# A four-layer network on one core: layer 0's scan taken two pixel tiles at a time, with its small work spread over other engines

## The chip, the cores and the metric

The kernel runs on one core of a Trainium2 chip. Five engines work side by side, each through its own queue in order: TensorE (PE; its weight loads are listed as PEld), VectorE (DVE), ScalarE (ACT), GpSimd (POOL) and SyncE (SP, which here only starts DMA transfers). The metric is the device time of the whole program in microseconds (us), as the median of several runs.

## The reference

One image x of 1024 channels by 64 x 64 pixels goes through four layers, each added to its input. Layer 0 is the one that changes:

```python
def layernorm2d(x):                       # over the 64 x 64 pixels of a channel
    return (x - mean) / sqrt(var + 1e-5) * w + b
x_norm = layernorm2d(group_norm(x))       # groups of 32 channels
dt     = softplus(einsum('bsdc,c->bsd', x_norm, dt_w) + dt_b)     # per channel s, image row d
log_a  = dt * -exp(log_A)
M      = exp(cumsum(log_a)[t] - cumsum(log_a)[j])  for j <= t, else 0
x      = x + einsum('btjr,bjrc->btrc', M, x_norm)
```

The sum over j with M is a recurrence along the channels: for each pixel, state[t] = exp(log_a[t]) * state[t-1] + x_norm[t]. Layer 1 is a group norm and a 1024 x 1024 product over the channels. Layer 2 has products, a scan whose order comes from sorting scores of the pixel positions, and gather and scatter by that order. Layer 3 is another 1024 x 1024 product.

## The kernel before

The products of layers 1 to 3 take nearly all the time, on TensorE. Layer 0 comes first and is all vector work. It is cut into 8 units, u = 0 to 7: unit u holds 256 channels (chunk c = u // 2, two tiles of 128 channels, k = 0 and 1) and half the image rows (h = u % 2), 2048 pixels. An even unit lies in a tile `low`, an odd one in `image`, which stays in SBUF for layer 1. A unit is worked in 4 pieces (g), a piece being 4 tiles of 128 pixels, so there are 32 pieces, i = 4u + g. A piece goes through these steps:

- unit_stats (L550): bn_stats on VectorE, 512 pixels each, 16 to a unit. norm_chunk (L558) makes a chunk's scale and bias: a chain VectorE, TensorE (L202), VectorE, TensorE (L211), VectorE, ScalarE (L172, L173), VectorE.
- normalize (L568): ScalarE writes xn, 1024 pixels at a time (L575).
- turn_in (L581): TensorE transposes eight 128 x 128 blocks into PSUM, so that pixels lie on partitions and channels along the row (L590). Four copies with weight and bias bring them to the piece's XT (10 buffers), on ScalarE (L598) or, for tiles named in `share`, on VectorE (L596).
- row_dt (L600): four matmuls sum a row's pixels with dt_w, into PD of the unit (L606). Each f32 matmul shows as two instructions.
- decay (L608), once per unit. Step 0: four ScalarE operations for the two parts of softplus (L615 to L618). Step 1: VectorE adds the parts (L621). Step 2: ScalarE makes a = exp(-exp(log_A) * dt) in PSUM (L624).
- scan (L626): four tensor_tensor_scan on VectorE, one for each pixel tile, over 256 channels (L632). From unit 2 on they start from `carry`, the last state of unit u - 2. hand_on (L635) copies the new last states to carry: VectorE for units 0 and 1, GpSimd after that (L638).
- turn_back (L641): TensorE transposes into two PSUM banks `pb` (L646). add_up (L649): VectorE adds each bank to the image in place and gives its sum for layer 1's norm (L656).
- squares (L659): ScalarE sums the squares for layer 1's variance, 1024 pixels at a time (L671), 512 in the last unit.

The order on VectorE, ScalarE, GpSimd, TensorE and SP is the program's own here (L513). The loop over the pieces (L722) is software-pipelined: in turn i it issues normalize(i+9), scan(i), hand_on(i), add_up(i-1), turn_in(i+7), row_dt(i+6), turn_back(i), then statistics of later units, a step of a norm chain, squares of the unit before, and a step of `sums`. The sums are GpSimd's: sums and differences of weight blocks for later layers (sum_weights, L440). They have a period of four pieces: at g = 0 four loads on GpSimd's queue (L448), at g = 2 four operations (L454 to L457), at g = 3 four stores (L460). The loads must wait for the stores before them.

Units come in by SP: cst and par (constants) first, then units 0 to 5 and 7; unit 6 at piece 8, when its buffer is free. The buffer is that of unit 0, whose result keep(0) writes out at piece 4. A table `spec`, which only layer 2 reads, is filled on GpSimd and stored by SP (L240) at the start. make_scores (L251) computes the positions' scores in small VectorE operations, in between the first norm chain and before it; sort_work (L328) sorts them during layer 1.

After the last piece, L770 to L775 make mean1 and var1, and pointwise (L952) the norm chain `gnl`. Then ScalarE writes normalized tiles (b, t; L948) for layer 1's matmuls (L844); VectorE makes differences of them (L802) and takes the products out of PSUM (L963, L967). Layer 1 has 56 products of eight matmuls, and the loop at L993 counts them as i. SP loads their weights (L827) into five buffers. In layer 1 only VectorE, TensorE, GpSimd and ScalarE keep the program's order; the scheduler places SP's transfers.

## Time and profile before

| | us |
|---|---|
| median of 3 runs (lowest, highest) | 2684.88 (2682.02, 2690.34) |
| the profiled execution | 2685.99 |
| its span in the trace | 2684.1 |
| first xn (L575) starts | 28.23 |
| first scans of pieces 0, 2, 4, 8, 12, 16, 20, 24, 28 start | 53.98, 69.31, 82.67, 102.65, 128.41, 149.56, 167.73, 185.42, 201.13 |
| last scan ends, layer 1's first matmul starts | 215.1, 225.07 |

Engine shares over the span: PE 96%, DVE 68%, ACT 40%, POOL 45%. In the profile's lines a group is: line, engine, operation, out<-in with shapes, count, busy us and mean ns of one, then idle time just before and who ended it. A timeline line gives start and duration in us, engine, line, operation, operands, count, and in brackets the wait before it with its releaser. Instructions of one engine overlap a little at their ends, so I take prices from the distance of starts. A stretch line gives its bounds, its length, each engine's busy us (and instructions), the granted TensorE clock, the DMA share and GB/s.

### The profile page before, as it was taken

The numbers are of one execution on the slowest core, as the hardware profiler recorded it, in microseconds if no ns is written. First come the engines' busy times: TensorE is split into PE (matmuls) and PEld (weight loads), VectorE is DVE, ScalarE is ACT, GpSimd is POOL, SyncE is SP. The second block draws the span as 40 slices with busy tenths as digits, with TensorE's granted clock in tenths as the row PEclk, the third lists the DMA queues.
The fourth block names the chain that finished last, engine by engine and source line by source line (L and its number), as shares of the span: only waits on it lengthen the run. The fifth ranks groups of instructions, "written<-read, shape, count | busy, mean of one in ns | idle before, by whom it ended". The sixth has DMA issues, their size and how long they took to land.

```text
span 2684.1 us, 30608 instructions
## 1 busy us (share of the span) xinstructions
PE 2564.7 (96%) x9520; PEld 1712.4 (64%) x9520; DVE 1833.2 (68%) x3870; ACT 1079.5 (40%) x1835; POOL 1215.3 (45%) x1100
## 2 busy tenths in 40 slices
PE   4788999999999999999999999999999999899998
PEld 3674444444555555444454448888888888788887
DVE  7996866655555564367787775677585775877877
ACT  3783110103556564466767663332233223312120
POOL 4154123242132243146474635566575565554544
PEclk9897999999999999999999999999999999999999
DMA  7245467547565577487667946889899798888896
GB/s 291 99 169 204 138 239 251 174 150 241 142 175 142 139 194 179 123 267 238 206 208 237 311 152 199 235 254 293 227 304 259 245 309 220 270 293 297 301 315 213
DMA packets 422741, 597.22 MB, mean 223 GB/s; under 512 B 141972, under 2 KB 210707, under 8 KB 419508
## 3 DMA queue, kind: packets, MB, share of 16 engines
q1 hardware_dynamic: 298020, 367.89, 43.4%
q10 hardware_dynamic: 91456, 136.33, 14.5%
q0 software_dynamic: 33104, 91.04, 13.3%
q8 instruction: 77, 1.26, 0.2%
q14 instruction: 84, 0.69, 0.1%
HBM read 435.10 MB, written 160.05 MB: 222 GB/s over the span
## 4 chain that ended last, share of the span: by engine, by line
PE 80%; DVE 10%; ACT 6%; DMA 2%; issue 1%; POOL 0%; DVEq 0%; ACTq 0%; SPq 0%; POOLq 0%
PE mm L844 36%; PE q_P5P L1728 5%; PE q_P6P L1728 5%; PE q_P7P L1728 5%; PE q_P3P L1728 5%; PE q_P4P L1728 5%; PE q_P2P L1728 5%; PE q_P1P L1728 5%; PE py L1375 2%; PE l2pt L1090 2%; DVE xt L632 1%; DVE cvp L1071 1%; DVE stats L554 1%; ACT b L948 1%; ACT xt L598 1%
## 5 line engine op out<-in xcount | busy, mean ns | idle before, releaser
L844 PE MATMUL mm<-t,w 128*128 128x512 f32 x1536 | 683.9, 596 | 0.0
L844 PE MATMUL mm<-b,w 128*128 128x512 f32 x1152 | 514.4, 598 | 4.0 <-ACT b L948 2.9
L844 PEld LDWEIGHTS mm<-t,w 128*128 128x128 f32 x1536 | 286.9, 191 | 323.1 <-issue 316.3
L844 PEld LDWEIGHTS mm<-b,w 128*128 128x128 f32 x1152 | 216.0, 191 | 252.3 <-issue 241.3
L1384 POOL DMA_INDIRECT y_rows<-g,dst x74 | 73.3, 990 | 184.3 <-ACT g L1380 171.7
L1071 DVE SCALAR_TENSOR_TENSOR cvp<-xs,par,cvp 128x512 f32<-128x512 f32 x128 | 95.3, 753 | 76.8 <-ACT cvp L1068 74.5
L1697 ACT COPY qQ<-q_P5P 128x512 f32<-128x512 f32 x48 | 28.1, 585 | 295.1 <-PE q_P5P L1728 288.8
L468 POOL TENSOR_TENSOR s<-s 128x256 f32<-128x256 f32 (+3 forms) x120 | 129.9, 1088 | 7.5
L1378 ACT COPY g<-py 8x512 f32<-8x512 f32 x146 | 83.8, 574 | 107.5 <-PE py L1375 101.7
L1122 DVE TENSOR_TENSOR xs<-mm,xs 128x512 f32<-128x512 f32 x64 | 41.8, 684 | 116.1 <-PE mm L844 116.1
L1098 POOL TENSOR_TENSOR acc<-l2xt,acc 128x136 f32<-128x136 f32 x56 | 27.8, 497 | 192.4 <-ACT l2xt L1092 191.4
L963 DVE SCALAR_TENSOR_TENSOR image<-mm,par,image 128x512 f32<-128x512 f32 x64 | 47.1, 746 | 96.4 <-PE mm L844 96.4
L1090 PEld LDWEIGHTS l2pt<-both,cv 128*128 128x128 f32 x512 | 76.3, 190 | 36.2 <-issue 22.5
L802 POOL TENSOR_TENSOR t<-t,b 128x512 f32<-128x512 f32 x40 | 55.7, 1419 | 91.8 <-DVE t L802 91.7
L1496 ACT ACTIVATE qb<-x_x_b,gn_bias,gn_r_r 128x512 f32<-128x512 f32 x64 | 48.8, 807 | 113.2 <-DVE qQ L1658 37.3
L948 ACT ACTIVATE b<-image,gnl_bias,gnl_r_r 128x512 f32<-128x512 f32 x48 | 37.2, 808 | 141.6 <-PE mm L844 113.3
L1728 PE MATMUL q_P1P<-t_b,wq_P1P 128*128 128x256 f32 x384 | 92.3, 385 | 1.5 <-POOL t_b L1492 1.5
L1728 PE MATMUL q_P4P<-t_t,wq_P4P 128*128 128x256 f32 x384 | 90.9, 380 | 1.4 <-DVE qV L1705 1.4
L1728 PE MATMUL q_P6P<-t_t,wq_P6P 128*128 128x256 f32 x384 | 90.8, 379 | 0.2 <-DMA wq_P6P<-s_d 0.2
L1728 PE MATMUL q_P5P<-t_t,wq_P5P 128*128 128x256 f32 x384 | 90.8, 379 | 0.0
L1728 PE MATMUL q_P7P<-t_t,wq_P7P 128*128 128x256 f32 x384 | 90.7, 379 | 0.0
L1728 PE MATMUL q_P2P<-t_b,wq_P2P 128*128 128x256 f32 x384 | 90.7, 379 | 0.0
(418 smaller groups left out, 5906.7 us busy)
## 6 DMA issues: line engine op xcount, KB each, us to landing
w<-s_d SPq DMA_DIRECT2D x96, 512.0 KB
w<-in_w_dram SPq DMA_DIRECT2D x72, 512.0 KB
x_x_b<-x_d ACTq DMA_DIRECT2D x28, 1024.0 KB
image<-x_d SPq DMA_DIRECT2D x12, 2048.0 KB
wq_P6P<-s_d SPq DMA_DIRECT2D x84, 256.0 KB
wq_P7P<-s_d SPq DMA_DIRECT2D x84, 256.0 KB
wq_P5P<-s_d SPq DMA_DIRECT2D x84, 256.0 KB
wq_P3P<-s_d SPq DMA_DIRECT2D x84, 256.0 KB
```

The costliest lines, as they stand in the source:

```text
L468: eng.tensor_tensor(out, a, b, ALU.subtract)
L802: eng.tensor_tensor(B[name][k], B[one][k], B[two][k], ALU.subtract)
L844: nc.tensor.matmul(to[o], w[:, k, o * P : (o + 1) * P], B[name][k], start=(fresh and k == 0), stop=(k == KH - 1), skip_group_check=True)
L948: nc.scalar.activation(t, X[nb][:, ct, :], AF.Identity, bias=bias, scale=scale)
L963: nc.vector.scalar_tensor_tensor(part, ps, pcol(bias_name, o), part, ALU.add, ALU.add)
L1071: nc.vector.scalar_tensor_tensor(cv, xo[:, at + t : at + t + FB], pcol("dww", 3 * o + t), cv, ALU.mult, ALU.add)
L1090: nc.tensor.matmul(pt[:, q * NV : (q + 1) * NV], cv[:, (q0 + q) * P : (q0 + q + 1) * P], both[:, o, :], start=True, stop=True)
L1375: nc.tensor.matmul(py, G2[k % 2], rows[k][:, :DH], start=True, stop=True)
L1378: nc.scalar.copy(rows[k + 1][h * LC : h * LC + S, :DH], py[h * LC : h * LC + S])
L1384: nc.gpsimd.indirect_dma_start(out=y_views[k % len(y_views)][:, :], out_offset=bass.IndirectOffsetOnAxis(ap=dst_[:, k : k + 1], axis=0), i ...
L1496: nc.scalar.activation(tile_of(j, name)[:, k], held[j, "x", name][:, k], AF.Identity, bias=bias, scale=scale)
L1728: nc.tensor.matmul(ps[:, o, :], w[:, k, o * P : (o + 1) * P], rhs[:, k, :], start=(new and o == 0 and k == 0), stop=(k == 1), skip_group_c ...
```

## The change

- The decay factor is written twice side by side into a PSUM tile `spread[h]` with column 0 of each half at zero. One scan then covers two pixel tiles, and the zero restarts it. Two scans of 512 a piece replace four of 256.
- The carried state is no longer the scan's start. GpSimd multiplies it by the factor of the unit's first channel (`first_`, a small ScalarE operation) and adds it to the first column of the unit's four XT tiles (begin). All hand_on copies are GpSimd's.
- Softplus's parts are added by two identity matmuls into the second half of PD's bank. decay's steps come one piece earlier: step 0 at g = 1, step 1 at the head of g = 2, step 2 at its end.
- For the last 7 pieces and k = 1, TensorE accumulates the image block (identity matmul) and the turned-back tiles in one bank, and ScalarE writes the sum to the image with its total.
- Squares take 2048 pixels at once, in two pieces of a unit. VectorE takes half of turn_in's copies for pieces 5 and 6, and in odd turns from 13 on. Statistics of units 7 and 6 lie in turns 4 to 7 and 9 to 11; unit 2's stand ahead of the first turn_in. bring(6) is in turn 5.
- Units 0 and 1 are loaded in four parts, the first ahead of par and cst. The scores, all but two small parts, come behind layer 1's norm chain, the sort begins in layer 1's turn 1, and the tables src, dst, diag and spec are made in its turn 20. Some memsets and sign changes go to GpSimd, and the copies of the mean come behind the norm chain.

```diff
@@
...
-    nc.sync.dma_start(cst, cst_d)
-    nc.sync.dma_start(par, par_d)
...
-    nc.vector.tensor_copy(src, cst[:, CST["from"]].to_broadcast([P, NK]))
-    nc.vector.tensor_copy(dst_, cst[:, CST["to"]])
-    nc.vector.tensor_scalar(diag, cst[:, CST["eye"]], pcol("D", 0), None, ALU.mult)
-    with tc.tile_pool(name="spec", bufs=1) as sp:
-        rows = sp.tile([NSPEC, DH + NF2], F32, name="spec")
+
+    def prepare_scan():
+
+        nc.vector.tensor_copy(src, cst[:, CST["from"]].to_broadcast([P, NK]))
+        nc.vector.tensor_copy(dst_, cst[:, CST["to"]])
+        nc.vector.tensor_scalar(diag, cst[:, CST["eye"]], pcol("D", 0), None, ALU.mult)
+        rows = sum1.tile([NSPEC, DH + NF2], F32, name="spec", bufs=1)
...
-        for u in (0, 1, 2, 3, 4, 5, 7):
+        bring(0, [0])
+        nc.sync.dma_start(par, par_d)
+        nc.sync.dma_start(cst, cst_d)
+        for u, k in ((1, 0), (0, 1), (1, 1)):
+            bring(u, [k])
+        for u in (2, 3, 4, 5, 7):
             bring(u)
...
+        nc.gpsimd.tensor_scalar(negA0, negA0, -1.0, None, ALU.mult)
+        nc.gpsimd.tensor_scalar(negA, negA, -1.0, None, ALU.mult)
...
+        nc.gpsimd.memset(sum0, 0.0)
+        nc.gpsimd.memset(sq0, 0.0)
+        spread = [ps0.tile([P, 2, CH * P], F32, name=f"a{i}", bufs=1) for i in range(2)]
+        first_ = [l0.tile([P, 1], F32, name=f"first{i}", bufs=1) for i in range(2)]
+        for a in spread:
+            nc.vector.memset(a[:, :, :1], 0.0)
...
+            norms[c] = yield from norm_steps(f"gn0_{c}", mean, var, CH, layernorm=True)
             nc.vector.tensor_copy(mean0[:, at], mean)
             nc.vector.tensor_scalar_mul(nmean0[:, at], mean, -1.0)
-            norms[c] = yield from norm_steps(f"gn0_{c}", mean, var, CH, layernorm=True)
...
             elif step == 1:
-                e, m = dt[u]
-                nc.vector.tensor_tensor(m, m, e, ALU.add)
+                for i, v in enumerate(dt[u]):
+                    nc.tensor.matmul(PD[u][:, CH * P :], ident, v, start=(i == 0), stop=(i == 1))
             else:
-                A[u] = ps0.tile([P, FB], F32, tag="a", name=f"a{u}")
-                nc.scalar.activation(A[u][:, : CH * P], dt[u][1], AF.Exp, scale=negA0[:, u % 2 : u % 2 + 1])
+                v, scale = PD[u][:, CH * P :], negA0[:, u % 2 : u % 2 + 1]
+                if u > 1:
+                    nc.scalar.activation(first_[u % 2], v[:, :1], AF.Exp, scale=scale)
+                nc.scalar.activation(spread[u % 2][:, :, 1:], v[:, 1:].unsqueeze(1).to_broadcast([P, 2, CH * P - 1]),
+                                     AF.Exp, scale=scale)
+
+        def begin(u):
+            h = u % 2
+            nc.gpsimd.tensor_scalar(carry[:, h], carry[:, h], first_[h], None, ALU.mult)
+            for g in range(NPIECE):
+                start = XT[NPIECE * u + g][:, :, 0]
+                nc.gpsimd.tensor_tensor(start, start, carry[:, h, 4 * g : 4 * g + 4], ALU.add)
...
         def scan(i):
-            for j in range(4):
-                xt = XT[i][:, j, :]
-                t = 4 * g + j
-                nc.vector.tensor_tensor_scan(xt, A[u][:, : CH * P], xt, carry[:, h, t : t + 1] if c else 0.0,
-                                             ALU.mult, ALU.add)
+            for j in (0, 2):
+                xt = XT[i][:, j : j + 2, :].rearrange("p t c -> p (t c)")
+                nc.vector.tensor_tensor_scan(xt, spread[h].rearrange("p t c -> p (t c)"), xt, 0.0, ALU.mult, ALU.add)
...
             if u + 2 < NU:
-                (nc.gpsimd if u > 1 else nc.vector).tensor_copy(
-                    carry[:, u % 2, 4 * g : 4 * g + 4], XT[i][:, :, CH * P - 1])
+                nc.gpsimd.tensor_copy(carry[:, u % 2, 4 * g : 4 * g + 4], XT[i][:, :, CH * P - 1])
+        def by_act(i, k):
+            return i >= NI - LEAD and k == 1
...
             for k in range(CH):
                 pb = ps0.tile([P, FB], F32, tag="pb", name=f"pb{i}_{k}")
+                if by_act(i, k):
+                    part = pieces_of(i, k)
+                    nc.tensor.matmul(pb.rearrange("p (j r q) -> p r q j", j=4, r=TR), ident, part, start=True, stop=False)
                 for j in range(4):
-                    nc.tensor.transpose(pb[:, j * P : (j + 1) * P], XT[i][:, j, k * P : (k + 1) * P], ident)
+                    at, xt = pb[:, j * P : (j + 1) * P], XT[i][:, j, k * P : (k + 1) * P]
+                    if by_act(i, k):
+                        nc.tensor.matmul(at, xt, ident, start=False, stop=j == 3)
+                    else:
+                        nc.tensor.transpose(at, xt, ident)
...
             for k in range(CH):
+                total = sum0[:, c * CH + k, at : at + 1]
+                if by_act(i, k):
+                    nc.scalar.activation(part, ps, AF.Identity, accum_out=total)
+                else:
+                    nc.vector.scalar_tensor_tensor(part, ps, 1.0, part, ALU.mult, ALU.add, accum_out=total)
...
+        def squares(u, k, g=None):
-            k, q = divmod(j, 2)
             ct = c * CH + k
-            junk = l0.tile([P, HN // 2], BF16, tag="junk", name=f"junk{u}_{j}_{g}", bufs=1)
-            if g is None:
-                part, at = half(u)[:, k, q * HN // 2 : (q + 1) * HN // 2], h * NPIECE + q
-            else:
-                part = half(u)[:, k, :].rearrange("p (r w) -> p r w", r=TR)[:, :, 16 * g : 16 * g + 16]
-                at = h * NPIECE + g
+            at = h * NPIECE + (g or 0)
+            junk = l0.tile([P, HN], BF16, tag="junk", name=f"junk{u}_{k}_{g}", bufs=1)
+            part = half(u)[:, k, :]
...
-        def score(n):
-            for _ in range(n):
-                next(scores, None)
-        score(18)
-        chain = norm_chunk(0)
-        for _ in range(3):
-            next(chain)
-            score(4)
-        finish_of(chain)
+        for k in range(CH):
+            unit_stats(0, range(4 * k, 4 * k + 4))
+            next(scores)
+            unit_stats(1, range(4 * k, 4 * k + 4))
+        finish_of(norm_chunk(0))
         for n in range(4):
             normalize(n)
-        unit_stats(2, range(4))
+        unit_stats(2, range(8))
         turn_in(0, range(4))
         turn_in(1, range(4), "pb")
-        for _ in scores:
-            pass
         row_dt(0)
-        turn_in(2, (1, 3))
+        turn_in(2, (2, 3))
         row_dt(1)
-        turn_in(3, (1, 3), "pb")
+        turn_in(3, (2, 3), "pb")
         row_dt(2)
-        unit_stats(2, range(4, 8))
         unit_stats(3, range(4))
         row_dt(3)
         decay(0, 0)
@@ -708,61 +730,67 @@
         decay(0, 2)
         next(chain)
         normalize(5)
+        next(chain)
         turn_in(4, ())
         next(chain)
         row_dt(4)
-        next(chain)
         normalize(6)
         normalize(7)
-        turn_in(5, ())
+        turn_in(5, (2, 3))
         row_dt(5)
-        turn_in(6, ())
-        todo = {0: [(4, range(4))], 1: [(4, range(4, 8))], 2: [(5, range(4))], 3: [(5, range(4, 8))],
-                8: [(7, range(4))], 9: [(7, range(4, 8))], 10: [(6, range(4))], 11: [(6, range(4, 8))]}
+        turn_in(6, (2, 3))
+        later = {}
+        for units, counts in (((4, 5), {0: 4, 1: 4, 2: 4, 3: 4}), ((7, 6), {4: 2, 5: 2, 6: 2, 7: 2, 9: 2, 10: 3, 11: 3})):
+            pieces = [(v, n) for v in units for n in range(8)]
+            for i, n in counts.items():
+                later[i] = [pieces.pop(0) for _ in range(n)]
         for i in range(NI):
             u, g = divmod(i, NPIECE)
             if i > 0 and i + LEAD + 2 < 4 * NU:
                 normalize(i + LEAD + 2)
+            if u + 1 < NU and g == 2:
+                decay(u + 1, 1)
             scan(i)
             hand_on(i)
             if i == 0:
                 finish_of(chain)
                 chain = iter(())
-            if g == 3 and u + 1 < NU:
-                decay(u + 1, 1)
-                decay(u + 1, 2)
             if i > 0:
                 add_up(i - 1)
             if i + LEAD < NI:
-                turn_in(i + LEAD, ())
+                turn_in(i + LEAD, (2, 3) if i > 11 and i % 2 else ())
             if i + LEAD - 1 < NI:
                 row_dt(i + LEAD - 1)
             turn_back(i)
             if i == 0:
                 normalize(LEAD + 1)
                 normalize(LEAD + 2)
+            if u + 1 < NU and g == 1:
+                decay(u + 1, 0)
             if u + 1 < NU and g == 2:
-                decay(u + 1, 0)
-            for v, some in todo.get(i, ()):
-                unit_stats(v, some)
+                decay(u + 1, 2)
+                if u > 0:
+                    begin(u + 1)
+            for v, n in later.get(i, ()):
+                unit_stats(v, (n,))
             if i in (3, 11):
                 chain = norm_chunk(2 if i == 3 else 3)
             next(chain, None)
-            if i >= NPIECE:
+            if i >= NPIECE and g < CH:
                 squares(u - 1, g)
             if u == NU - 1 and 0 < g:
                 for k in range(CH):
-                    squares(u, 2 * k, g - 1)
+                    squares(u, k, g - 1)
             if g == 0 and u % 2 == 1:
                 last_keep = keep(u // 2)
-            if i == 2 * NPIECE:
+            if i == NPIECE + 1:
...
-    def pointwise(name, m, bias_name, order, src, dst):
+    def pointwise(name, m, bias_name, order, src, dst, meanwhile):
         norm = {}
         columns(range(CT), finish_of(norm_steps(f"gn{name}", mean1, var1)), norm)
+        for _ in range(22):
+            next(meanwhile)
         def before(pair):
...
-        for i, _ in enumerate(pointwise("l1", W1, "b1", [3, 2] + EARLY, x0_d, x1_d)):
+        for i, _ in enumerate(pointwise("l1", W1, "b1", [3, 2] + EARLY, x0_d, x1_d, scores)):
             busy = next(sums, None) if i % 14 < 13 else None
+            if i == 1:
+                for _ in scores:
+                    pass
+                coming[0] = next(order)
+            if i == 20:
+                prepare_scan()
```

## The prediction

> **What bounds the kernel now.** I read the chain of waits first, to see whether layer 0 is on the path at all.
>
> ```profile
> PE 80%; DVE 10%; ACT 6%; DMA 2%; issue 1%; POOL 0%; DVEq 0%; ACTq 0%; SPq 0%; POOLq 0%
> ```
>
> TensorE carries 80%. The same view cut to the first 420 us shows that the rest is mostly layer 0, which ends at 225.07 us with layer 1's first matmul; behind that TensorE is gapless. So a microsecond taken from layer 0 is a microsecond of the kernel. Next came the busy time per stretch, cut at the units' first scans (engine busy in us, then TensorE clock, DMA share, GB/s):
>
> ```profile
> 0.00:28.20 28.20, 1.44 (x5) 1.06 (x5) 19.94 (x72) 2.40 (x7) 15.10 (x31) 1.00 0.93 357
> 28.20:54.00 25.80, 17.56 (x79) 15.15 (x80) 19.06 (x39) 12.99 (x19) 11.83 (x14) 0.89 0.80 326
> 102.60:128.40 25.80, 16.54 (x99) 13.21 (x97) 25.71 (x53) 22.05 (x41) 10.17 (x16) 0.97 0.45 164
> 149.60:167.70 18.10, 16.77 (x100) 13.85 (x100) 15.81 (x33) 18.07 (x34) 10.86 (x18) 1.00 0.36 128
> 201.10:218.50 17.40, 9.40 (x40) 7.40 (x38) 16.65 (x38) 11.16 (x24) 6.61 (x11) 0.50 0.88 334
> ```
>
> The bound moves: the load first, VectorE in unit 2 (25.71 of 25.80), ScalarE in unit 4 (18.07 of 18.10), VectorE at the end, where TensorE runs at half clock. The timeline shows the hand-overs:
>
> ```profile
> 17.45 4.84 DVE L554 BATCH_NORM_STATS2 stats<-image 128x6 f32<-128x512 f32 x8 [0.66 <-DMA image<-in_x_dram]
> 26.72 1.26 POOL L454 TENSOR_TENSOR s_s<-s_a,s_a 128x512 f32<-128x512 f32 x1 [9.83 <-DMA s_a<-in_w_dram]
> 26.76 1.24 DVE L177 SCALAR_TENSOR_TENSOR gn_r_r<-gn_r_t,gn_r_r 128x2 f32<-128x2 f32 x1
> 53.98 2.42 DVE L632 TENSOR_TENSOR_SCAN xt<-a,xt 128x256 f32<-128x256 f32 x4
> 65.70 0.69 DVE L656 SCALAR_TENSOR_TENSOR low<-pb,low 128x512 f32<-128x512 f32 x1 [3.53 <-PE pb L646]
> 165.03 0.60 DVE L621 TENSOR_TENSOR m<-m,e 128x256 f32<-128x256 f32 x1 [1.44 <-ACT e L618]
> 167.73 2.67 DVE L632 TENSOR_TENSOR_SCAN xt<-a,carry,xt 128x256 f32<-128x256 f32 x4 [0.88 <-ACT a L624]
> ```
>
> Eight statistics run only after unit 1 has landed whole; a 2-element L177 takes 1.24 us beside a GpSimd operation; the first addition waits 3.53 us for TensorE; at each unit's end VectorE waits for the softplus.
>
> **What the Trainium skill says.** "SBUF — State Buffer", Who interferes with whom: a VectorE instruction with two SBUF inputs and a GpSimd one that reads SBUF exclude each other for a whole instruction. The trace agrees (L177 against L454). "TensorE: Matmul & The Clock Gate", Part 1: the clock is either full or half, by recent activity; Part 4: transposes don't count as activity. It agrees: with transposes alone the clock was 0.50 (201.10:218.50), with row_dt's matmuls among them 1.00. "ScalarE: Activation LUTs", What ACT_TABLE_LOAD costs: about 0.28 us plus 0.833 ns an element; here 128x1024 squares took 1.146 and 128x512 0.722, a slope of 0.83 ns.
>
> **The change part by part.** Sums are against the profiled execution, 2685.99 us (span 2684.1).
>
> *Prices.* From starts in the timeline: scan of 256 0.605 (four in 2.42), 0.645 with a carry; addition 0.61; statistic 0.605; xt on ScalarE 0.465, on VectorE 0.47; xn 1.13; a 1024 square with its accumulator read 1.13; turn_in 0.97, row_dt 1.89, turn_back 0.87 at full clock. A scan of 512 isn't shown. "VectorE: DVE Perf Modes", Specifications, gives 0.96 GHz: a 512 statistic is then 0.533 + 0.07 us, and the 256 scan, as long, takes two cycles an element. Bounds: 1.07 (no fixed cost) to 1.21 (twice 0.605); I take 1.14, so 2.28 a piece against 2.42 or 2.59. A 2048 square: 2 x 1.13 less one fixed 0.28 = 1.99 (bounds 1.7 and 2.26). Spread exponential of 510: 0.40 + 0.25 = 0.65, with first_ 0.2. Softplus on TensorE: two f32 matmuls of 256, each two passes as in row_dt, 4 x 0.236 = 0.94.
>
> *Start.* Four 1 MB loads, and constants second. By 11.5 us the DMA view's slices make 3.4 MB at some 380 GB/s, and 4.8 MB are needed; GpSimd's weight loads, issued from 14.46, now come after hand_on(0). I put the last landing at 15.7 (bounds 14.8 and 17.4), statistics' end 2.42 later at 18.1, against 22.29. The chain from there to the first xn took 5.9; the mean copies (0.33), the score operations between (0.4) and L177's stall (1.1) go: 4.1. First xn at 22.2, not 28.2: **-6.0**. The removed VectorE constants and scores ran while it waited for loads: nothing.
>
> *Up to the third scan.* Unit 2's eight statistics (4.84) now stand ahead of the xt evacuations, so XT0 is 1.1 later after xn0. Then the softplus no longer waits for statistics (2.45 at L624), and gn_pv no longer stands behind turn_in(4). But VectorE's halves of pieces 5 and 6 now precede scan(0): they need row_dt(4), turn_in(5), row_dt(5), turn_in(6), which ends 31 us behind xn0. Then scan, 0.7 chain, 2.42 statistics, scan, 1.22 additions, 2.42: scan(2) at 42.4 behind xn0, formerly 41.1. At 64.6, not 69.3: **-4.7 in all**. First scan is thus hardly earlier; what goes is the 3.53 wait.
>
> *Pieces 2 and 3:* 2.28 + 1.22 + 2.42 each, 0.5 aggregate: 12.4 for 13.4, **-1.0**. *4 to 7* (statistics of unit 7 moved here from 8 and 9): 4 x 3.5, eight statistics 4.84, norm chain 2.0: 20.8 for 20.0, **+0.8**. *8 to 11:* 14.0 + 4.84 + 0.5, some slack: 19.6 for 25.8, **-6.2**; ScalarE needs xt 4 x 1.87 = 7.5, xn 4 x 1.13 = 4.5, squares 2 x 1.99 = 4.0, softplus 1.5 and exponentials 0.85: 18.4, so it doesn't decide. *12 to 15:* VectorE 14.0 + two half evacuations 1.9 + chain 2.0 = 18.0 for 21.1, **-3.1**. *16 to 23:* per unit ScalarE 18.4 less the 1.9 of xt that VectorE takes = 16.5, VectorE 14.0 + 1.9 = 15.9, TensorE 4 x 3.73 + 0.94 = 15.9: three within 4%, so I take 17.0 twice for 35.9, **-1.9**. *24 to 27:* two at 3.5, two at 2.9: 12.8 for 15.7, **-2.9**. *28 to 31:* ScalarE with four additions of 0.85, two squares of 1.99, six of 0.85: 12.5 for 14.0, **-1.5**. *Tail:* identity matmul 0.9 and four two-pass matmuls 1.04 behind the last scan, then ScalarE's addition: **+0.7**; at half clock +2.5.
>
> *Hidden, and the new waits.* begin is one product and four additions at about 0.2 each, as the carry copy's 0.19: 1.1 us on GpSimd. It waits for first_ and for the last hand_on; behind it stand the 5.3 us of weight sums; the unit's first scan waits for it. It is issued two pieces (8 us) ahead, so it costs nothing unless GpSimd, blocked at L448 for stored weights (2.67 at the longest within the loop), reaches it over 7 us late; then the excess is paid six times. TensorE's softplus waits for ScalarE's Ln with turn_in(i+7) behind it; the spread exponential waits for TensorE with squares and the next xn behind it. Both engines have 1 to 2 us in such a piece, since the scan that needs the result is two pieces off. The eight idle spells before L624 (14.4 us in all) go; what is late next there is ScalarE itself. VectorE's L596 waits for turn_in, with the next scan behind it: TensorE does it during the scan before (0.97 in 2.28). bring(6) moves three pieces up SP's queue and waits for keep(0) and the squares of unit 0; nothing follows on SP until keep(1), and its data are wanted at piece 9: nothing. The 22 score operations, some 4 us, lie in VectorE's 9.34 wait at layer 1's start. prepare_scan: 0.7 us each on VectorE and GpSimd in layer 1's slack; its store joins SP's weight queue.
>
> Sum: -19.8, so 2666.2; the median shown lies 1.1 below that execution: **2665**.
>
> **Rivals.** *TensorE and hand-overs bind.* With three equal engines in order, VectorE's half evacuations wait for TensorE, which waits for ScalarE; gaps bring half clock (0.79 in the fourth unit before). For: those gaps, 131 to 136. Against: 1.00 in units 4 and 5. Units 3 to 5 at 18.5 to 19.5 lose 5, the end at half clock 4: 2674.
>
> *More goes than I count.* Loads land at 14.8, unit 2 isn't slowed at the start, and units 4 and 5 reach 16.5: 2657.
>
> *Gain lost to coupling everywhere:* units at their old length except 2: about 2680, no change.
>
> *Slower: SP is held by the spec store.* L240 stands on SP, in order, and waits for GpSimd. Before, it delayed SP only until 5.15. At layer 1's i=20 SP also feeds weights, and GpSimd waited up to 30.33 us for s_a there. Five weight buffers last five products of 3.43 us, 17 us, less about 4 for landing: 13 are free. The excess is paid 1:1 by TensorE. It decides beyond 13 + 20 + 8 = 41 us of blocking; at 48 the excess is 35, so 2700. Against: nothing obliges the store to stand far ahead in SP's order.
>
> **How the numbers follow.** Forecast 0.58, alone 2658 to 2672; TensorE and hand-overs 0.20; more 0.12; coupling 0.05; SP 0.05. 0.3% is 8 us, about what a measurement of this kernel tells from no change. Faster: all but little of the forecast, three quarters of the second, all of the third: 0.86; same 0.09; slower 0.05. The range 2654 to 2678 leaves out parts of the outer cases.
>
> **What would show it.** The first xn near 22; scan(2) near 65; scans of 1.14 us; no VectorE wait before a unit's first scan; unit 2 near 19.6; layer 1's first matmul near 205, TensorE gapless after it. A carry wait ahead of a unit's first scan, half clock in units 3 to 5, or an SP gap near 275 to 300 would prove the forecast wrong.

## The result and the profile after

The changed kernel took 2667.5 us (median of 6 runs, 2666.57 to 2672.35) against 2683.47 us for the kernel before in the same runs: a ratio of 0.9939, 95% interval 0.9928 to 0.9949, so 0.61% faster. The forecast was 2665.0, with a range of 2654 to 2678. The profiled execution took 2667.54 us, span 2665.8, where the one before had 2685.99 and 2684.1: 18.3 us of span, against a forecast of 19.8. Of the 18.3, layer 0 gave 16.3 (its end, layer 1's first matmul, moved from 225.07 to 208.76); the other 2.0 lie in the code behind it, which the forecast left as it was.

Line numbers from here on are those of the changed kernel, unless "before" is said: L585 is normalize; L600 turn_in's transposes, with its copies to XT on VectorE (L606, called half evacuations below) and ScalarE (L608); L616 row_dt; L628 the logarithm of softplus and L631 the addition behind it; L641 and L644 begin; L651 the scan; L677 turn_back's transposes, L671 and L675 the identity matmul and the accumulating matmuls of the last seven pieces; L691 and L689 the additions on VectorE and ScalarE; L170 to L220 the norm chains; L440 to L460 GpSimd's weight sums, as before. Unit u is pieces 4u to 4u + 3.

The chain of waits of the changed kernel, the line of shares by engine:

```profile
PE 84%; DVE 7%; ACT 6%; issue 1%; DMA 1%; POOL 1%; SPq 0%; DVEq 0%; ACTq 0%; POOLq 0%
```

VectorE's share fell from 10 to 7, and GpSimd (POOL), at 0 before, now has 1%. Next the busy time per stretch of the changed kernel, cut at the units' first scans (PE, PEld, DVE, ACT, POOL busy, then TensorE clock, DMA share, GB/s):

```profile
0.00:21.80 21.80, 1.18 (x4) 1.00 (x4) 13.28 (x41) 2.40 (x7) 10.35 (x25) 1.00 0.93 374
96.75:116.15 19.40, 16.95 (x111) 15.40 (x110) 19.15 (x35) 19.37 (x34) 12.30 (x23) 1.00 0.42 155
116.15:137.85 21.70, 17.37 (x99) 15.09 (x98) 17.27 (x41) 16.57 (x29) 9.93 (x21) 0.92 0.53 194
137.85:154.20 16.35, 15.41 (x102) 14.06 (x101) 15.81 (x30) 16.23 (x28) 10.96 (x22) 1.00 0.37 130
186.25:197.10 10.85, 7.16 (x35) 5.00 (x33) 10.85 (x15) 6.42 (x11) 7.67 (x11) 0.84 0.81 279
```

Unit 2 (96.75 to 116.15) is 19.4 us long, not 25.8, and ScalarE and VectorE both fill it. Unit 4 (137.85 to 154.20) has three engines within 6% of each other, ScalarE first with 16.23 of 16.35. Between them stands unit 3, in which no engine is busy for more than 17.4 of its 21.7 us and the clock is 0.92: nobody's work sets it. The last unit belongs to VectorE alone. The timeline of the changed kernel shows the hand-overs (start, length, engine, line, in brackets the idle time before and who ended it):

```profile
15.28 2.47 DVE L564 BATCH_NORM_STATS2 stats<-image 128x6 f32<-128x512 f32 x4
...
51.65 2.33 DVE L651 TENSOR_TENSOR_SCAN xt<-a,xt 128x512 f32<-128x512 f32 x2
...
127.43 0.99 DVE L606 TENSOR_SCALAR xt<-xpt,par 128x256 f32<-128x256 f32 x2 [1.91 <-PE xpt L600]
...
186.24 2.34 DVE L651 TENSOR_TENSOR_SCAN xt<-a,xt 128x512 f32<-128x512 f32 x2 [3.03 <-POOL xt L644]
...
203.76 0.22 DVE L798 TENSOR_REDUCE mean<-sum 128x8 f32<-128x64 f32 x1 [2.83 <-ACT image L689]
```

The last statistics start at 15.28 with no wait for a transfer. Two scans of 512 take 2.25 us from the start of the first to that of the next instruction, 1.12 each. Before scan(28) VectorE stands for 3.03 us because GpSimd has not yet added the carried states (L644), and the mean over the image waits 2.83 us for ScalarE's last addition.

I laid the starts of scans 0, 4, 8 and so on of both profiles beside the forecast (us; "0 to 3" is from the start of scan(0) to that of scan(4), and so on; the "tail" is from the end of scan(31) to layer 1's first matmul):

| stretch | before | forecast | after |
|---|---|---|---|
| first xn at | 28.23 | 22.2 | 21.81 |
| scan(0) at | 53.98 | 53.2 | 51.65 |
| pieces 0 to 3 | 28.69 | 23.8 | 23.39 |
| 4 to 7 | 19.98 | 20.8 | 21.71 |
| 8 to 11 | 25.76 | 19.6 | 19.41 |
| 12 to 15 | 21.15 | 18.0 | 21.68 |
| 16 to 23 | 35.86 | 34.0 | 32.71 |
| 24 to 27 | 15.71 | 12.8 | 15.69 |
| 28 to 31 | 14.03 | 12.5 | 10.85 |
| tail | 9.91 | 10.6 | 11.67 |
| layer 1's first matmul at | 225.07 | 205.3 | 208.76 |
| from there to the end | 2459.0 | 2459.0 | 2457.0 |

So the start, units 0 and 2, units 4 and 5 and the last unit gave what was forecast or more. Unit 1 took 1.7 us where 0.8 was forecast, units 3 and 6 gave nothing, and the tail took 1.8.

### The profile page after: what moved, and what is told of

The parts are those of the page before. It is cut to its first block, busy times and chain, and to the rows that moved or that the text cites. A ratio compares the mean times of both kernels' runs of the same rounds, so it can differ in the third digit from the quotient of the medians.

```text
span 2665.8 us, 30739 instructions
## 1 busy us (share of the span) xinstructions
PE 2569.6 (96%) x9594; PEld 1717.6 (64%) x9594; DVE 1819.2 (68%) x3790; ACT 1075.3 (40%) x1811; POOL 1222.6 (46%) x1142
## 4 chain that ended last, share of the span: by engine, by line
PE 84%; DVE 7%; ACT 6%; issue 1%; DMA 1%; POOL 1%; SPq 0%; DVEq 0%; ACTq 0%; POOLq 0%
PE mm L872 38%; PE q_P2P L1763 5%; PE q_P6P L1763 5%; PE q_P5P L1763 5%; PE q_P3P L1763 5%; PE q_P7P L1763 5%; PE q_P1P L1763 5%; PE q_P4P L1763 5%; PE l2pt L1125 2%; PE py L1410 2%; ACT b L976 1%; DVE cvp L1106 1%; PE pd L616 1%; DVE xt L651 1%; DVE stats L564 1%
## 5 line engine op out<-in xcount | busy, mean ns | idle before, releaser
L1133 POOL TENSOR_TENSOR acc<-l2xt,acc 128x136 f32<-128x136 f32 x56 | 29.3, 523 | 191.7 <-ACT l2xt L1127 184.6
L1527 POOL TENSOR_TENSOR t_t<-qt 128x512 f32<-128x512 f32 x23 | 29.6, 1288 | 134.0 <-DVE qt L1527 74.2
L1740 DVE TENSOR_TENSOR qZ<-q_P6P,qZ 128x512 f32<-128x512 f32 x96 | 64.7, 685 | 38.4 <-PE q_P6P L1763 38.1
## 6 DMA issues: line engine op xcount, KB each, us to landing
image<-x_d SPq DMA_DIRECT2D x12, 2048.0 KB, 12.8
```

The lines of the kernel that those rows point to most:

```text
L1740: nc.vector.tensor_tensor(to, ps, to, ALU.add)
```

## The experiments

All experiments are edits of the changed kernel. The code from layer 1's first matmul on is the same in all of them, and yet it took between 2453.3 and 2464.1 us in their profiled executions. Whole times therefore say little below 3 us, and I judge by the stretches of layer 0. Pieces 0 to 3, 8 to 11 and 16 to 23 repeat within 0.1 us wherever an edit doesn't touch them (pieces 16 to 23: 32.6 to 32.7 in eleven of the twelve profiles where VectorE keeps its half evacuations). The others are less steady: the last two runs are the same program up to piece 30, and pieces 4 to 7 took 21.11 and 21.87 in them; with nothing changed in them, pieces 12 to 15 were once 1.0 shorter (no additions elsewhere), pieces 24 to 27 took 14.4 (old loads) to 16.7 us (last addition back), and the tail 13.2 with the old loads. There, and in the sum, one profile doesn't show a difference of 1 us. The stretches are counted from scan(0), because the time from the first xn to scan(0) itself varied between 29.3 and 30.9; the sum goes to layer 1's first matmul:

| run | 0-3 | 4-7 | 8-11 | 12-15 | 16-23 | 24-27 | 28-31 | tail | sum | ratio to before [95%] |
|---|---|---|---|---|---|---|---|---|---|---|
| changed kernel | 23.39 | 21.71 | 19.41 | 21.68 | 32.71 | 15.69 | 10.85 | 11.67 | 157.1 | 0.9939 [0.9928, 0.9949] |
| four scans | 23.76 | 21.70 | 19.43 | 21.77 | 32.69 | 15.24 | 11.24 | 11.67 | 157.5 | 0.9943 [0.9927, 0.9960] |
| softplus on VectorE | 23.74 | 24.84 | 20.87 | 22.31 | 33.61 | 13.66 | 10.84 | 11.88 | 161.8 | 0.9954 [0.9937, 0.9971] |
| no additions elsewhere | 23.40 | 21.87 | 19.38 | 20.67 | 32.69 | 14.99 | 12.69 | 8.50 | 154.2 | 0.9933 [0.9916, 0.9950] |
| no half evacuations | 23.39 | 21.28 | 19.40 | 20.00 | 36.65 | 13.18 | 10.86 | 11.66 | 156.4 | 0.9954 [0.9938, 0.9971] |
| sums later | 23.40 | 21.74 | 19.40 | 21.67 | 32.71 | 13.25 | 10.85 | 12.94 | 156.0 | 0.9941 [0.9924, 0.9957] |
| old loads | 23.39 | 21.57 | 19.40 | 21.68 | 32.71 | 14.36 | 10.85 | 13.23 | 157.2 | 0.9945 [0.9929, 0.9962] |
| old statistics | 23.39 | 20.23 | 23.81 | 20.20 | 32.70 | 14.91 | 10.85 | 16.42 | 162.5 | 0.9934 [0.9915, 0.9952] |
| norm chain first | 24.69 | 20.35 | 21.72 | 18.36 | 32.69 | 13.98 | 10.86 | 16.30 | 159.0 | 0.9939 [0.9922, 0.9955] |
| sums sooner | 23.39 | 21.34 | 19.38 | 21.68 | 32.69 | 14.25 | 10.85 | 13.24 | 156.8 | 0.9938 [0.9917, 0.9959] |
| last addition back | 23.39 | 21.78 | 19.39 | 21.67 | 32.69 | 16.67 | 11.42 | 10.11 | 157.1 | 0.9934 [0.9919, 0.9949] |
| three edits | 23.40 | 21.11 | 20.50 | 16.78 | 32.62 | 13.32 | 10.85 | 11.60 | 150.2 | 0.9922 [0.9908, 0.9935] |
| three edits, five pieces | 23.39 | 21.87 | 20.48 | 16.78 | 32.61 | 13.15 | 10.86 | 8.90 | 148.0 | 0.9895 [0.9878, 0.9912] |

**Four scans.**

```diff
-            for j in (0, 2):
-                xt = XT[i][:, j : j + 2, :].rearrange("p t c -> p (t c)")
-                nc.vector.tensor_tensor_scan(xt, spread[h].rearrange("p t c -> p (t c)"), xt, 0.0, ALU.mult, ALU.add)
+            for j in range(4):
+                xt = XT[i][:, j, :]
+                nc.vector.tensor_tensor_scan(xt, spread[h][:, 0, :], xt, 0.0, ALU.mult, ALU.add)
```

> The changed kernel with one thing undone: four scans of 256 a piece instead of two of 512 (over the first half of the same spread factor; carries by GpSimd stay). Scans then take 2.42 us a piece, where two of 512 took 2.25. Theory 'VectorE's own work sets most pieces': pieces 0 to 11 and 28 to 31 longer by 0.17 each, 16 pieces, +2.7 us in all, and nothing in pieces 12 to 27, where ScalarE, TensorE or GpSimd came last. Rival 'VectorE sets every piece': +5.4 (32 x 0.17). Rival 'hand-overs bind, the scan's price hardly matters': under +1.

Pieces 0 to 3 grew by 0.37 us, 28 to 31 by 0.39, 12 to 15 by 0.09; the others did not grow, and unit 6 with its wait for the carry was 0.45 shorter. In sum +0.4, in the steady stretches 0.8: either way the rival holds. The two-tile scan, the first item in the change's name, is worth under 1 us by itself, for two reasons. The scans set the time in two units only. And the price was too high: 2.42 is the time from the start of the first scan to the end of the fourth, while up to the start of the next instruction the four take 2.35, against 2.25 for the two:

```profile
187.24 2.43 DVE L651 TENSOR_TENSOR_SCAN xt<-a,xt 128x256 f32<-128x256 f32 x4 [2.20 <-POOL xt L644]
189.59 0.67 DVE L691 SCALAR_TENSOR_TENSOR low<-pb,low 128x512 f32<-128x512 f32 x1
```

Four times 0.10 is what each of the two units grew by.

**Softplus on VectorE.**

```diff
-                for i, v in enumerate(dt[u]):
-                    nc.tensor.matmul(PD[u][:, CH * P :], ident, v, start=(i == 0), stop=(i == 1))
+                e, m = dt[u]
+                nc.vector.tensor_tensor(m, m, e, ALU.add)
...
-                v, scale = PD[u][:, CH * P :], negA0[:, u % 2 : u % 2 + 1]
+                v, scale = dt[u][1], negA0[:, u % 2 : u % 2 + 1]
```

> The changed kernel with the softplus' addition back on VectorE (128x256, 0.60 us, once in a unit), two pieces ahead of the scan that needs it; the exponential then reads SBUF. Theory 'it was the place in the order that cured the waits, not the engine': +0.6 us in each unit where VectorE comes last (units 1, 2 and 7), under +0.6 in the others, together +2 to +4, with no wait over 0.3 us before L633. Rival 'VectorE waits for the logarithm again': 1 us or more before each, +8 to +12. Rival 'nothing': within 0.5.

VectorE's timeline of this run, three of its six waits at the addition:

```profile
91.42 0.43 DVE L631 TENSOR_TENSOR m<-m,e 128x256 f32<-128x256 f32 x1 [3.86 <-ACT e L628]
...
111.43 0.43 DVE L631 TENSOR_TENSOR m<-m,e 128x256 f32<-128x256 f32 x1 [1.39 <-ACT e L628]
...
136.11 0.43 DVE L631 TENSOR_TENSOR m<-m,e 128x256 f32<-128x256 f32 x1 [2.09 <-ACT e L628]
```

Six waits of 0.65 to 3.86 us, 9.5 in all, cost 4.6 us from scan(0) to layer 1's first matmul (6.5 up to scan(24); unit 6, with a shorter wait for the carry, was 2.0 quicker). My theory's "no wait over 0.3" was wrong, its size a little low; the rival had the mechanism right, and twice the size. At this place in the order, then, it is the engine that counts: the addition holds its engine's queue while ScalarE finishes the logarithm. In the changed kernel TensorE waits at L631 instead, up to 2.45 us in a unit, and that costs less than the waits of VectorE. The addition on TensorE at its old place was not run.

**No additions elsewhere.** `by_act` returns False.

> The changed kernel with all additions back on VectorE (no identity matmul, no addition by ScalarE in the last seven pieces). Theory 'the relief of VectorE and the longer tail nearly cancel': pieces 24 to 27 unchanged at 15.7 us, since VectorE waited 3.03 us for the carry there and has room for 3 x 0.61; pieces 28 to 31 from 10.8 to 13.2 (4 x 0.61); the tail from the end of scan(31) to the mean from 6.7 to about 3.5; together -0.8 us. Rival 'the relief is worth its forecast' (2.9 + 1.5 less 0.7): slower by 3 to 4. Rival 'TensorE was held up by the accumulating matmuls all along': faster by 3 or more.

Unit 6 lost 0.7 us, unit 7 took 1.84 more, the tail 3.2 less: 2.9 us faster than the changed kernel. Expected was -0.8: the tail is as expected, only three of the four additions lie within pieces 28 to 31, and unit 3, which the edit doesn't touch, happened to lose 1.0 less; the 0.7 of unit 6 is no more than such chance either. In the changed kernel, then, the relief of VectorE brought nothing: unit 6 waits for GpSimd anyway, and the tail gives back more than unit 7 gains. The windows of this run over unit 7 and from the last scan to the mean (same columns as above):

```profile
185.55:198.25 12.70, 6.19 (x26) 4.71 (x24) 12.70 (x21) 7.45 (x12) 7.70 (x11) 0.50 0.78 274
198.25:201.70 3.45, 1.94 (x8) 1.57 (x8) 2.60 (x9) 2.43 (x6) 0.00 (x0) 0.50 0.99 376
```

TensorE is at half clock throughout, and that costs nothing while VectorE is busy for all 12.70.

**No half evacuations.** `turn_in(i + LEAD, ())` in all turns of the loop; pieces 5 and 6 keep theirs.

> The changed kernel with ScalarE doing all of xt (VectorE evacuates no half from piece 12 on). Theory 'the new waits of VectorE for TensorE cost unit 3 its gain, but ScalarE needs the help in units 4 and 5': pieces 12 to 15 from 21.7 to about 20, pieces 16 to 23 from 32.7 to 35 to 36 (ScalarE has 1.9 more a unit), together +1 to +2 us. Rival 'the halves are what lost unit 3': pieces 12 to 15 at 18, the others unchanged, -3. Rival 'the halves don't matter': within 0.5.

Pieces 12 to 15 fell by 1.7 us, 16 to 23 rose by 3.9, +2.3 together, a little more than the theory had; then VectorE, being later, met a carry that was nearly ready (a wait of 0.51 us), and unit 6 gave 2.5 back, so that the sum is no longer than the changed kernel's. The windows of units 4 and 5 of this run show who sets them:

```profile
135.30:154.40 19.10, 16.66 (x101) 14.92 (x100) 14.09 (x25) 19.07 (x32) 12.01 (x25) 0.91 0.32 111
154.40:171.95 17.55, 15.70 (x103) 14.32 (x103) 14.31 (x27) 17.02 (x30) 9.96 (x19) 1.00 0.65 239
```

ScalarE is busy for 19.07 of 19.10: these two units need the half evacuations.

**Old loads.** Constants first, units 0 and 1 in one load each, statistics unit by unit.

```diff
-        bring(0, [0])
-        nc.sync.dma_start(par, par_d)
         nc.sync.dma_start(cst, cst_d)
-        for u, k in ((1, 0), (0, 1), (1, 1)):
-            bring(u, [k])
-        for u in (2, 3, 4, 5, 7):
+        nc.sync.dma_start(par, par_d)
+        for u in (0, 1, 2, 3, 4, 5, 7):
             bring(u)
...
-            unit_stats(0, range(4 * k, 4 * k + 4))
-            next(scores)
-            unit_stats(1, range(4 * k, 4 * k + 4))
+            unit_stats(k, range(8))
+            next(scores)
```

> The changed kernel with the loads in their old order: constants, then units 0 and 1 in one load each, and the statistics unit by unit. Theory 'the start is on the path in full': the eight statistics of unit 1 start when it has landed whole, at 17.4 us, and end at 22.3; the first normalised tile comes at 26.4 instead of 21.8, and layer 1's first matmul 4 to 4.6 us later. Rival 'the next loads take over': with the start later the waits behind it (VectorE's 5.57 and 2.14 us for TensorE before the first scan) shrink, and under 2 us are lost at layer 1.

The first xn came at 26.74, 4.93 us later than in the changed kernel, and layer 1's first matmul at 213.6, 4.84 later; from scan(0) to scan(24) the stretches are the same within 0.15. The sums are equal too, but only because unit 6 was 1.3 shorter and the tail 1.6 longer, which the edit doesn't explain. The start is on the path nearly in full. Of the 6.4 us that it gained, the order of loads and statistics is 4.9. By subtraction the remaining 1.5 belong to what left the norm chain: the scores, the mean copies and the stall at L177 of the kernel before. They were not undone one by one.

**Old statistics.** Unit 7's and unit 6's statistics in pieces 8 to 11, four in each, none in 4 to 7.

> The changed kernel with unit 7's and unit 6's statistics back in pieces 8 to 11, four in each (none in 4 to 7). Theory 'the gain of pieces 8 to 11 is the statistics that left them, and where they went costs less': pieces 8 to 11 from 19.4 to 24.2 (eight of 0.605 more), pieces 4 to 7 from 21.7 to 18.4 at best (ScalarE's work), together +1.5 us. Rival 'VectorE comes last in both, so statistics can be moved at no gain': 4 to 7 at 16.9, together 0. Rival 'the move is worth nearly all that pieces 8 to 11 gained': 4 to 7 stay above 20, together +3.5 or more.

Pieces 8 to 11 grew by 4.40, 4 to 7 fell by 1.48 and 12 to 15 by 1.48, so +1.4 from scan(4) to scan(16), what the theory gave. Where VectorE was not the bound, the statistics cost a third of their time. The sum is 5.4 longer, though, because the tail is 4.75 longer. VectorE's timeline at layer 1's norm chain in this run shows 2.05 of that:

```profile
210.72 1.27 DVE L173 TENSOR_TENSOR gnl_r_t<-gnl_r_r 128x8 f32<-128x8 f32 x1 [0.52 <-ACT gnl_r_r L171]
212.02 0.17 DVE L174 SCALAR_TENSOR_TENSOR gnl_r_t<-gnl_r_t,gnl_v 128x8 f32<-128x8 f32 x1
212.22 1.12 DVE L175 SCALAR_TENSOR_TENSOR gnl_r_r<-gnl_r_t,gnl_r_r 128x8 f32<-128x8 f32 x1
```

L173 and L175 have two SBUF inputs of eight elements and take 1.27 and 1.12 us. GpSimd's weight sums run from 210.71, and both end with one of them; L174, of the same size, started in the gap between two sums and took 0.17. In the changed kernel the chain ended 2.7 us before those sums began, and the two instructions took 0.17 each. The rest of the 4.75 is TensorE at half clock in the last two pieces. The next run has a tail as long with the statistics in their new place, so the long tail is not the price of the old ones.

**Norm chain first.** The bank of the group sums (L200) is one of the two that turn_in uses. In the changed kernel its reader L203 is queued behind scan(12) and two additions:

```profile
119.75 0.75 PE L600 MATMUL xpt<-cst,xn 128*128 128x128 f32 x4 [2.05 <-DVE gn_d L203]
120.34 2.86 PE L616 MATMUL pd<-xt,dtm 128*128 128x256 f32 x8
```

TensorE's transposes of piece 19 wait 2.05 us for it, and row_dt after that took 2.86 us where it takes 1.89 at full clock. The edit:

```diff
+            if i > 0:
+                next(chain, None)
             scan(i)
...
                 chain = norm_chunk(2 if i == 3 else 3)
-            next(chain, None)
+                next(chain)
```

> The changed kernel with each step of the norm chains of pieces 4 to 7 and 12 to 15 ahead of the piece's scan instead of at the piece's end, so that the bank of the group sums is read before TensorE needs it for turn_in. Theory 'that bank held up TensorE in unit 3': the 2.05 us wait of TensorE for L203 in piece 12 goes, TensorE stays at full clock, VectorE's waits of 1.75 and 1.91 behind it shrink, and pieces 12 to 15 take 19 to 20 us instead of 21.7. Rival 'VectorE's wait for the group sums takes its place': no gain, or up to 2 us lost. Rival 'unit 3 is bound by ScalarE': within 0.5 of 21.7 with waits for ScalarE.

A step now stands ahead of a unit's first scan, so the boundaries move; pieces 8 to 15 together took 40.08 us against 41.09, a gain of 1.0 where 1.7 to 2.7 was expected. VectorE and TensorE in this run:

```profile
117.34 1.15 DVE L205 TENSOR_TENSOR gn_d<-gn_d,gn_mv 128x2 f32<-128x2 f32 x1
118.54 0.38 PE L209 MATMUL gn_pv<-gn_d,cst 128*128 128x2 f32 x2 [1.62 <-DVE gn_d L205]
```

The two-element L205 took 1.15 us beside GpSimd's L457 (117.21 to 118.47), and TensorE, whose next matmul needs it, waited 1.62 us in place of 2.05; row_dt behind it still took 3.41. The bank was the first cause, and the sums on GpSimd took its place.

**Sums later and sums sooner.** In the changed kernel GpSimd's order in unit 6 is: stores of a group, loads of the next, begin(7). Its timeline:

```profile
182.45 0.54 POOL L448 DMA_DIRECT2D s_a<-in_w_dram  x1 [1.37 <-DMA s_d<-s_a]
183.96 1.59 POOL L448 DMA_DIRECT2D s_a<-in_w_dram  x3 [0.97 <-DMA s_d<-s_a]
185.59 0.34 POOL L641 TENSOR_SCALAR carry<-carry,first 128x16 f32<-128x16 f32 x1
186.01 0.71 POOL L644 TENSOR_TENSOR xt<-xt,carry 128x4 f32<-128x4 f32 x4
```

The loads wait twice for stores to land, and begin(7), the carry's addition (L641, L644), stands behind them. Two edits put begin ahead of the loads:

```diff
-            next(sums, None)
+            if i > 1:
+                next(sums, None)
```

> The changed kernel with GpSimd's weight sums started two pieces later, so that the carried states of a unit are added ahead of a group's weight loads and not behind them. Theory 'unit 7 waits for GpSimd, which is held at the weight loads': the 3.03 us wait of VectorE for L644 before scan(28) goes, pieces 24 to 27 take 12.7 to 13.5 instead of 15.7, layer 1 starts 2 to 3 us earlier, and nothing else moves. Rival 'another engine is as late': under 1 us gained, with a wait of scan(28) for ScalarE or TensorE in its place. Rival 'the later sums run into the end': GpSimd's last stores come after layer 0's end and layer 1's first products are late, 0 or slower.

```diff
-            next(sums, None)
+            for _ in range(1 if i else 3):
+                next(sums, None)
```

> The changed kernel with GpSimd's weight sums two pieces sooner (three steps of them after piece 0 instead of one), which also puts a unit's carried states ahead of a group's weight loads, but lets the last sums end within layer 0. Theory 'unit 7 waits for GpSimd held at the loads, and starting the sums later only moved them into layer 1's norm chain': no wait over 0.7 us before scan(28), pieces 24 to 27 at about 13.2 us (15.7 in the changed kernel), the stretch from the end of the last scan to layer 1's first matmul at 11.7 (12.9 with the sums later), layer 1's first matmul 2 to 2.5 us earlier counted from the first scan. Rival 'the weights' traffic is late whatever the order': the carry still comes late in unit 7, or the first unit's transfers are delayed, under 1 us.

The wait before scan(28) went from 3.03 to 0.59 us with the sums later and to 1.58 with them sooner, and pieces 24 to 27 from 15.69 to 13.25 and 14.25. But the tail took 1.3 and 1.6 us of it back. Neither gained the 2 to 3 us expected: what unit 6 gave was lost behind it. (With the sums sooner the carry still came 1.58 us late, as its rival had it.) In both, TensorE's identity matmul of piece 30 waited 2.12 us (1.15 in the changed kernel, where TensorE was late itself), and matmuls after it ran at half clock (L675 of piece 30 in 1.90 and 1.60 us instead of 1.05). A quick unit 6 doesn't bring this about by itself: with no half evacuations unit 6 took 13.18, and the tail 11.66. What separates the profiles is how long TensorE had gone without an accumulating matmul, doing only transposes or waiting. From the end of piece 29's L675 to L671 of piece 30 it was 3.21 us in the six profiles in which L675 of piece 30 then took 1.57 to 1.91, and 1.3 to 2.3 in the five in which it took 1.05.

**Last addition back.** `by_act` excludes i = 31.

> The changed kernel with the last piece's second addition back on VectorE (six pieces keep it on TensorE and ScalarE). Theory 'the identity matmul, the accumulating matmuls and ScalarE's addition, one after another in piece 31, make the long tail': from the end of the last scan to layer 1's first matmul 9.0 us instead of 11.7, pieces 24 to 31 unchanged, 2 to 3 us gained. Rival 'the tail comes from piece 30's addition, which holds the accumulator bank': 11 or more, under 1 gained.

The tail fell by 1.56 us to 10.11, between theory and rival. The sum didn't move, since unit 6's wait for the carry was 4.01 us this time (begin(7) at 187.17). The edit changes nothing before piece 31; GpSimd's round began 1.0 us later in this execution, counted from scan(0), and why is open.

**Three edits, and five pieces.** The sums sooner, the last addition back, the norm chain first in pieces 12 to 15 only; then the same with ScalarE's additions in pieces 25 to 29 only.

> The changed kernel with three edits together: weight sums two pieces sooner, the last piece's second addition on VectorE, and the norm chain of pieces 12 to 15 ahead of each scan (that of pieces 4 to 7 as it was). Theory 'three separate losses': pieces 12 to 15 about 1 us shorter with their boundary, 24 to 27 at 13.2, the tail at 9.0; layer 1's first matmul at 202 to 203.5 instead of 208.8, the whole 0.2% below the changed kernel, 2661 to 2663. Rival 'what one gives another takes': the first matmul above 206.

> The kernel of the run with three edits, with ScalarE's additions in pieces 25 to 29 only: both additions of the last two pieces on VectorE. In the run with three edits TensorE's identity matmul of piece 30 waited 2.12 us for a VectorE addition queued behind scan(31), and TensorE went through the tail at a clock of 0.75. Theory 'piece 30's identity matmul holds up the tail': piece 30's extra addition falls behind the last scan in any case, so pieces 24 to 31 stay at 13.3 and 10.9 us, the stretch from the end of the last scan to layer 1's first matmul goes from 11.6 to about 8.5, as it was with all additions on VectorE, and the first matmul comes at about 198. Rival 'the slow clock makes the tail': transposes alone leave TensorE at half clock, and the stretch stays above 11. Whole: 2659 to 2661 by the theory, 2663 by the rival.

With three edits, the whole took 2663.3 us, just above the theory's 2661 to 2663, and layer 1's first matmul came at 201.23 us, earlier than the theory had it. Unit 3 gave 3.8 us and not 1: pieces 8 to 15 took 41.09 us in the changed kernel, 41.05 with the sums sooner alone, 40.08 with the norm chain first alone, and 37.28 with both. The two losses hid each other. With the sums sooner, no sum runs beside L205:

```profile
115.98 0.16 DVE L205 TENSOR_TENSOR gn_d<-gn_d,gn_mv 128x2 f32<-128x2 f32 x1
116.20 0.38 PE L209 MATMUL gn_pv<-gn_d,cst 128*128 128x2 f32 x2 [0.64 <-DVE gn_d L205]
```

The same L205 takes 0.16 us, TensorE waits 0.64 for it, and row_dt stays at 1.89. The tail was still 11.60. TensorE's timeline in this run, from piece 30 on:

```profile
187.53 0.63 PE L677 MATMUL pb<-cst,xt 128*128 128x128 f32 x4 [0.46 <-DVE image L691]
190.28 1.27 PE L671 MATMUL pb<-image,cst 128*128 128x512 f32 x2 [2.12 <-DVE image L691]
191.34 1.91 PE L675 MATMUL pb<-cst,xt 128*128 128x128 f32 x8
193.05 1.06 PE L677 MATMUL pb<-cst,xt 128*128 128x128 f32 x4
```

The identity matmul of piece 30 waits 2.12 us for an addition of VectorE that stands behind scan(31), and what follows runs at half clock, L675 in 1.91 and not 1.05. With five pieces the tail is 8.90, near the 8.5 of the theory, and the rival's "above 11" falls. The first matmul came at 201.04 and not 198, since in that profile scan(0) was 1.95 us later and pieces 4 to 7, the same code, took 0.76 more. The wait itself is still there:

```profile
192.79 1.09 PE L677 MATMUL pb<-cst,xt 128*128 128x128 f32 x8 [2.12 <-DVE image L691]
```

Piece 30's plain transposes wait the same 2.12 us. What the edit took away is the work behind the wait, L671 and L675, and not the wait. The windows of this run over unit 7 and from the last scan to the mean:

```profile
181.30:192.15 10.85, 7.97 (x46) 5.46 (x44) 10.85 (x15) 8.55 (x17) 6.20 (x10) 1.00 0.85 318
192.15:196.00 3.85, 2.01 (x12) 1.37 (x12) 2.60 (x9) 3.65 (x11) 3.57 (x6) 0.80 0.96 373
```

It took 2657.3 us against 2685.1, a ratio of 0.9895 [0.9878, 0.9912], whose interval lies wholly below that of the changed kernel. Against the run with three edits the intervals overlap; there the stretches decide, with a tail 2.7 us shorter.

## Why the prediction was right, point by point

The total was 2.5 us low (2665.0 against 2667.5), and it is that near by luck in part. Layer 1's first matmul was forecast at 205.3 and came at 208.76. Stretches that were worse than forecast lost 8.6 us, above all units 3 and 6; those that were better gave back 5.1; and 2.0 came from the code behind layer 0, within its spread from one execution to the next. Two of the signs that the prediction named as proof against itself appeared, a carry wait ahead of a unit's first scan and half clock in unit 3.

*Start, -6.0:* measured -6.4, by the order of loads (4.9) and, by subtraction, the cleared norm chain (1.5). The landing that I put at 15.7 was never waited for; the statistics ended at 17.66, near the 18.1 of the sum, and the chain took the 4.1 us given. Scan(2) came at 62.90 for 64.6.

*Pieces 2 to 11:* -1.0, +0.8 and -6.2 were forecast, -1.2, +1.7 and -6.4 measured. The old statistics confirm the step: they cost 4.4 us in unit 2 and saved 1.5 on each side.

*The scan:* 1.14 predicted, 1.12 measured. But the price of the old one, 0.605, is a quarter of the 2.42 from the first start to the last end; from starts a scan of 256 without a carry took 0.58, so the saving is 0.10 a piece and not 0.14. The term counted it in every piece, too, and the runs give it under 1 us in all. What the two-tile scan makes possible, carries off VectorE, was not tested apart.

*Pieces 12 to 15, -3.1: failed,* measured +0.5, 3.7 us more than forecast. The step "VectorE 14.0 + two half evacuations 1.9 + chain 2.0 = 18.0" added up one engine's work. It left out that the chain's group sums lie in a bank of turn_in, read only after the scan and the additions. The rival "TensorE and hand-overs bind" names this: TensorE waited, its clock fell, and VectorE's next addition and its new evacuation waited for it, 1.75 and 1.91 us: the 3.7. It happened in one unit of three. The three edits took 16.78 us here (37.28 with the unit before, against 37.6 in the forecast): the sum of work was right, and the hand-over was missing (and with it GpSimd's hold on L205).

*Pieces 16 to 23, -1.9:* measured -3.2. The three engines were within 6%, but hardly any of it was lost in hand-overs: 16.35 a unit, where I took 17.0 and ScalarE's own sum was 16.5.

*Pieces 24 to 27, -2.9: failed,* measured 0. The step "it costs nothing unless GpSimd, blocked at L448 for stored weights, reaches it over 7 us late; then the excess is paid six times" had the mechanism and the place. The excess was paid once, 3.03 us, before unit 7. My reading, not tested apart, is that only in unit 6 do the pieces (12.7 us without the wait) become quicker than GpSimd's round of sums, stores and loads (14.75 us from one L454 to the next in the changed kernel, at 173.47 and 188.22). It stood in the working as a bound, and in none of the rivals.

*Pieces 28 to 31, -1.5:* measured -3.2. VectorE comes last at 2.84 a piece, and ScalarE doesn't: the forecast gave it 12.5 us of work there, and it was busy for 6.42 of 10.85. Its addition took 0.57 us and not 0.85, and three of its additions and most of the small squares fell behind the last scan, into the tail. So the two terms belong together: -0.8 forecast, -1.4 measured.

*Tail, +0.7: the term that was mis-sized.* It measured +1.8, or +3.27 up to the mean with 1.5 regained in the norm chain, where a stall of 1.1 us at L771 of the kernel before, beside GpSimd, was gone. The sum counted piece 31's own matmuls. It did not count piece 30's identity and accumulating matmuls, which start only when VectorE is past scan(31), nor the second wait of 0.79 at piece 31. The records name VectorE's addition of the same piece as what L671 waits for, and the bank or the image could be behind it. In the five-piece run transposes that read no image waited as long, so the image isn't needed for the wait; what holds the bank until then is open.

*Hidden:* right, but for begin. The scores ran in layer 1's start, TensorE has no wait from its first matmul there to 420 us, prepare_scan cost nothing visible; the rival in which SP is held fell. "Coupling everywhere" fell too. One reading was wrong without harm: the 14.4 us of idle time before L624 were four spells, not eight.

The clock in the last unit answers what the prediction cited from "TensorE: Matmul & The Clock Gate", Part 4: with transposes alone it was 0.50 (185.55 to 198.25, no additions elsewhere), with the accumulating matmuls 1.00 (181.30 to 192.15, five pieces). And the L205 and L173 stalls fit what it cited from "SBUF — State Buffer", Who interferes with whom: 1.15 and 1.27 us beside a GpSimd sum, 0.16 and 0.17 without.

## What to carry to other kernels

Where three engines are in balance, add up each engine's work and then ask, for every buffer they share, what the reader is queued behind: a small read behind a long scan cost more here than doubling the scan gained. When one wait goes and little is gained, look for a second that it hid: of two edits, one alone gave 1.0 us, the other nothing, and both together 3.8. An operation moved off the bound engine pays only where that engine has more to do behind it, so don't move it in the last pieces. Judge an edit of a microsecond by the stretch that it touches, since the rest of a long kernel moves by more than that from one execution to the next, and first see in the other runs how far that stretch moves by itself.

## What the runs showed of the hardware

The same code behind layer 0 took 2453.3 to 2464.1 us in thirteen profiled executions of the changed kernel and its edits, while a stretch such as pieces 16 to 23 repeated to 0.1 us in eleven of them. Scans of 256 took 0.58 us each from start to start and scans of 512 took 1.12, so little is saved by joining two. An eight-element VectorE instruction with two SBUF inputs took 0.17 or 1.27 us by whether a GpSimd sum ran beside it. In the last seven pieces TensorE's clock fell by how long it had done nothing but transposes and waiting. Where it had been at full clock, gaps of up to 2.3 us between two pieces' accumulating matmuls left the next eight at 1.05 us, gaps of 3.07 us and more made them 1.5 to 1.91, and of two gaps between, 2.45 us did and 2.52 did not. So in the tail a wait cost more than its length. At layer 0's end GpSimd waited 7.81 us for its stores of weights to land in the changed kernel, where the same wait had been 1.2 to 5.6 us in the units before.
